# A hand-written order around the last attention tiles and the first expert blocks: two schedule strings rewritten

## The chip, the cores and the metric

The kernel runs on one core of one Trainium2 chip. The metric is the device time of one execution in microseconds; a kernel's time is the median of its runs.

## What is computed

The reference is one block of a Perceiver-like network in float32, on 64 sequences of 32 tokens of 256 features (2048 tokens), each sequence with its own context of 257 rows of 128 features. Cut to what matters:

```python
x = x + cross_attention(layernorm(x), ctx)       # 16 heads of 64; keys and values from ctx
x = x + self_attention(layernorm(x))             # 4 heads of 64, rotary angles, 32 tokens a sequence
x = x + experts(layernorm(x))                    # 8 experts, the best 2 of each token

# experts: scores = x @ Wr.T + br; top 2; their softmax weights, normalized to sum 1
# h = x @ Wl1[e]; y = (silu(h[:, :512]) * h[:, 512:]) @ Wl2[e]; out = weighted sum of the two y
```

## The kernel before

**Tiles.** The 2048 tokens are 16 tiles of 128 tokens, four sequences each. For every sequence, `cross_probs` computes scores, softmax and a transpose, in four steps (named `s` in the schedule). `cross_mix`, named `mix`, multiplies the probabilities of a pair of sequences with the context's values. The rest of a tile is a generator, `rest`: output of the cross attention, self-attention, routing. The generator yields at places where TensorE would have to wait for another engine, so that another piece of work can be put in between.

**The pipeline.** While tile t goes through scores and mixes, the `rest` of tile t-1 is called `near`, that of t-2 `far` and that of t-3 `late`. `ahead` computes the queries of tiles to come. A string for each sequence of a tile tells which generator makes its next step, word by word; `last_steps` holds the four strings of tile 15. After its last mix there is no tile left to compute scores for: `near` is then the rest of tile 15, `far` that of tile 14.

**Experts.** Each token goes to two of eight experts. `route` finds them and scatters the token's row into a DRAM tensor `routed` by indirect DMAs from GpSimd, two for a tile; the second waits for the first. Blocks of 128 rows of one expert are then gathered from `routed`. Six "early" blocks hold only rows that were routed by tile 12, so they can run while tiles 14 and 15 are still in their `rest`. `late_blocks` counts the rows of all tiles and lays out the late blocks (28 run for this input). A block has these units in the schedule:

- `x`, `prepared`: the gathered rows are transposed (by TensorE, L752, for early blocks and the first eight late ones), and VectorE forms gates and targets (L762 to L768).
- `a`, `first_half`: 8 matmul calls (L783), the halves that go through silu.
- `b`, `second_half`: 8 more; ScalarE's silu (L801), VectorE's product (L806).
- `c`, `combined`: 4 matmul calls (L818), bias and gate on VectorE (L823, L824), then an indirect DMA by GpSimd that adds the rows into `out` (L825).

The first layer's bias is read from the weights by L801 and L806, the second layer's by L823; weights stay in "lanes" of SBUF, two for early blocks (even blocks in lane 0, odd ones in lane 1) and three for late ones. After `c` of block b, SyncE issues the loads for block b + 2, under a condition that is true if the expert differs.

**What sets the order.** TensorE and SyncE (with its DMA queue) execute in the program's order, as the code writes it: `tc.manual_schedule(engines={SP, PE})`. VectorE, ScalarE and GpSimd execute in an order that a scheduler chooses when the program is built, and each of them in that order strictly. A reordering of the strings thus changes TensorE's order as written and the others' as the scheduler finds. PSUM has eight banks; `banks` gives out the one that was taken longest ago, and `a` holds its bank until `b`. The tiles `bxT` have two buffers, `y` four.

**Lines that come up.** L238 and L239: transposes on TensorE and their copies. L359, L363, L364, L371, L373: scores, maximum, exp, normalizing, transpose. L390 mix. L414, L428, L432, L438 output of the cross attention (L424 and L422 copy its middle). L221 to L231 layer norm, with a power on GpSimd (L228, `rstds` before self-attention, `rstdr` before routing). L448, L451 to L464 query, key and value and their rotation. L478, L485, L486, L494 to L503 scores and softmax of the self-attention, whose transposed probabilities are `diag`. L508, L516, L519, L522, L523 its output. L556 to L622 routing (`rex`, L587, is a power on GpSimd for the last two tiles, L619 their store to `out`). L647, L649 counts for the late blocks; `meta` (L908, L911, L918) tells SyncE which rows and weights to fetch.

Of the kernel before, what the change touches and what calls it, by code (L numbers as in the profile page):

```python
# [51 lines left out]
def block_kernel(  # L52
# [880 lines left out]
    def rotary_tables():  # L933
# [87 lines left out]
        "late ahead late s near s near s far s mix",  # L1021
    )
    last_steps = (
        "late far ahead s late far s s near s",
        "s near late far late s s s near ahead far mix ahead",
        "s s far s near s far",
        "s s near s near s mix far",
    )
    probs = {}
    seqs = [(t, b) for t in range(NT) for b in range(4)]  # L1030
# [19 lines left out]
    def iota(shape, pattern, base, by_partition, name):  # L1050
        it = const.tile([P] + shape, FP, name=name)
        nc.gpsimd.iota(
            it,
            pattern,
            base=base,
            channel_multiplier=by_partition,
            allow_small_or_imprecise_dtypes=True,
        )
        return it
# [21 lines left out]
    late = iota([LATE], [[1, LATE]], 0, 0, "late")  # L1081
# [38 lines left out]
    for n, (t, b) in enumerate(seqs):  # L1120
# [19 lines left out]
        if n + 1 < len(seqs):  # L1140
            t1, b1 = seqs[n + 1]
# [42 lines left out]
    def do(units):  # L1184
        for unit in units.split():
            if unit in work:
                next(work[unit], None)
            else:
                b = int(unit[1:])
                {  # L1190
                    "x": blocks.prepared,
                    "a": blocks.first_half,
                    "b": blocks.second_half,
                    "c": blocks.combined,
                }[unit[0]](b)
                if unit[0] == "c" and b + 2 < EARLY:
                    blocks.weights(b + 2, (0, 1))

    do("x0")
    blocks.gathered(EARLY - 1)  # L1200
    do("near far near far near a0 far x1 b0 near far near near x2 c0 near a1 near far b1 far")
    do("a2 near c1 far near x3 b2 a3 near c2 near x4 b3 near a4")
    late, total = late_blocks(done)
    do("c3")
    for b in range(3):
        late.gathered(b)
    do("b4 x5 a5 c4")
    late.weights(1, (0, 1))
    do("b5")
    late.prepared(0)  # L1210
    early_ones, blocks = blocks, late

# [107 lines left out]
```

## Time and profile before

| what | us |
|---|---|
| median of 3 runs (767.99 to 773.94) | 769.27 |
| the profiled execution, its own time | 770.71 |
| its span, first to last instruction | 768.9 |
| TensorE busy (8402 matmul instructions) | 726.0 |
| VectorE, ScalarE, GpSimd busy | 507.9, 394.0, 322.7 |

The profile is of one execution. Each call of a float32 matmul shows as two matmul records. In timeline rows the columns are start, duration, engine, line, operation, output and inputs, and in brackets the idle time before with what ended it. In rows of stretches the columns are the stretch, its length, the busy time (and instructions) of TensorE, its weight load, VectorE, ScalarE and GpSimd, the granted TensorE clock as a share of full speed, the DMA engines' busy share and GB/s. In the chain of work that ended last, each row is start, duration and what the end was waiting on at that time.

### The profile page before, as it was taken

Reading aid. Unit: us, or ns where it says so; the run is one execution under the profiler, and the core shown is the slowest. Engines: PE = TensorE matmul, PEld = TensorE weight load, DVE = VectorE, ACT = ScalarE, POOL = GpSimd, SP = SyncE. Lnnn points to the kernel's source line nnn. Section 1 sums busy time; section 2 is a strip of 40 time slices with the busy share of each in tenths; the row PEclk is TensorE's granted clock in tenths of the full one; section 3 lists DMA queues with packets and bytes.
Section 4 is the critical chain, followed back from the end, with each engine's and each line's share of the span. In section 5 each row is a group of like instructions: output and inputs, shape, how many; then the busy total and the mean of one; then the engine's idle time right before and its main releaser. Section 6 shows DMA issues by size and latency. Waiting matters only on the chain.

```text
span 768.9 us, 22412 instructions
## 1 busy us (share of the span) xinstructions
PE 726.0 (94%) x8402; PEld 616.3 (80%) x8402; DVE 507.9 (66%) x1968; ACT 394.0 (51%) x1168; POOL 322.7 (42%) x598
## 2 busy tenths in 40 slices
PE   8889999999999999999999999999698999999990
PEld 7668888787788878888787787887587999999990
DVE  4648777777886887787688777896267344454440
ACT  3756666666666676666666666764232222212210
POOL 2101072845648376474745738211135123322331
PEclk9999999999999999999999999999899999999996
DMA  8884323443333343233433334427212984485421
GB/s 247 229 213 106 90 78 88 122 113 93 92 87 112 88 134 100 77 94 98 120 107 86 91 88 115 124 84 259 105 11 60 329 300 56 51 251 114 57 36 22
DMA packets 62335, 90.85 MB, mean 118 GB/s; under 512 B 24144, under 2 KB 49104, under 8 KB 60688
## 3 DMA queue, kind: packets, MB, share of 16 engines
q1 hardware_dynamic: 55696, 80.32, 36.4%
q0 software_dynamic: 6528, 9.06, 6.6%
q8 instruction: 68, 1.11, 0.6%
q14 instruction: 43, 0.35, 0.2%
HBM read 113.76 MB, written 13.16 MB: 165 GB/s over the span
## 4 chain that ended last, share of the span: by engine, by line
PE 57%; POOL 13%; DVE 11%; DMA 9%; issue 5%; SPq 2%; ACT 1%; POOLq 0%; DVEq 0%
PE psum L783 13%; PE psum L359 9%; PE psum L390 8%; PE psum L818 6%; PE psum L432 5%; PE psum L334 5%; POOL rprod L544 4%; POOL rprod L539 4%; PE psum L448 3%; PE psum L313 3%; DMA out_x<-y_late,to_late 2%; SPq L101 2%; DVE prT L373 2%; DMA routed<-xr,rslots 2%; PE psum L414 1%
## 5 line engine op out<-in xcount | busy, mean ns | idle before, releaser
L364 ACT ACTIVATE pr<-psum,nmx 128x257 f32<-128x257 f32 x256 | 120.3, 474 | 90.2 <-DVE nmx L363 88.5
L359 PE MATMUL psum<-kvT,q 128*128 128x257 f32 x512 | 142.3, 399 | 3.4 <-DMA kvT<-in_ctx_t 2.3
L390 PEld LDWEIGHTS psum<-prT,kvA 32*128 32x128 f32 x4096 | 118.1, 187 | 11.2 <-issue 4.7
L390 PE MATMUL psum<-prT,kvA 32*128 32x128 f32 x4096 | 124.8, 274 | 0.5 <-ACT pr L364 0.4
L363 DVE TENSOR_REDUCE nmx<-psum 128x1 f32<-128x257 f32 x256 | 104.5, 414 | 30.3 <-PE psum L359 28.8
L371 ACT ACTIVATE pr<-pr,inv 128x256 f32<-128x256 f32 x256 | 114.7, 503 | 14.8 <-DVE inv L369 14.6
L359 PEld LDWEIGHTS psum<-kvT,q 128*128 128x128 f32 x512 | 89.6, 192 | 27.4 <-issue 7.9
L373 DVE STREAM_TRANSPOSE prT<-pr 128x512 f32<-128x512 f32 x128 | 89.9, 703 | 20.9 <-ACT pr L371 19.6
L825 POOL DMA_INDIRECT out_x<-y_late,to_late x28 | 43.6, 1558 | 109.3 <-DMA out_x<-y_late,to_late 43.0
L544 POOL TENSOR_TENSOR rprod<-rprod 128x128 f32<-128x128 f32 x192 | 75.3, 392 | 14.3
L539 POOL TENSOR_TENSOR rprod<-xr,wr_row 128x256 f32<-128x256 f32 x96 | 69.9, 728 | 7.5 <-DVE xr L231 0.8
L398 ACT COPY cT<-psum 128x512 f32<-128x512 f32 x64 | 34.2, 586 | 68.6 <-PE psum L390 68.6
L783 PE MATMUL psum<-bxT_late,lane 128*128 128x128 f32 x576 | 69.3, 275 | 0.0
L783 PEld LDWEIGHTS psum<-bxT_late,lane 128*128 128x128 f32 x576 | 68.2, 192 | 1.1 <-issue 0.2
L334 PE MATMUL psum<-xqT,xwq_sb 128*128 128x256 f32 x256 | 60.8, 381 | 0.5 <-ACT xqT L239 0.5
L432 PE MATMUL psum<-xwo_sb,ov 128*128 128x256 f32 x256 | 60.1, 382 | 0.5 <-DVE ov L424 0.2
L432 PEld LDWEIGHTS psum<-xwo_sb,ov 128*128 128x128 f32 x256 | 48.1, 190 | 9.1 <-DVE ov L424 2.9
L334 PEld LDWEIGHTS psum<-xqT,xwq_sb 128*128 128x128 f32 x256 | 48.6, 191 | 8.0 <-ACT xqT L239 0.7
L801 ACT ACTIVATE sag_late<-psum,lane 128x128 f32<-128x128 f32 x72 | 20.5, 368 | 63.9 <-PE psum L783 63.9
L364 ACT ACTIVATION_READ_ACCUMULATOR pr<-psum,nmx 128x1 f32 x256 | 50.9, 199 | 0.0
L611 POOL DMA_INDIRECT routed<-xr,rslots x32 | 33.0, 1032 | 41.0 <-DMA routed<-xr,rslots 23.7
L406 POOL TENSOR_TENSOR xb<-x,xbo_bc 128x256 f32<-128x256 f32 x16 | 11.6, 728 | 87.4 <-DVE x L438 62.6
(268 smaller groups left out, 1204.0 us busy)
## 6 DMA issues: line engine op xcount, KB each, us to landing
kvA<-in_ctx_a SPq DMA_DIRECT2D x256, 128.0 KB
lane<-in_wall SPq DMA_DIRECT2D x24, 1028.0 KB
lane<-in_wall SPq DMA_DIRECT2D x24, 640.0 KB
lane2a<-in_wall SPq DMA_DIRECT2D x10, 1028.0 KB
kvT<-in_ctx_t SPq DMA_DIRECT2D x64, 128.5 KB
lane2b<-in_wall SPq DMA_DIRECT2D x10, 640.0 KB
xg_late<-routed SPq DMA_DIRECT2D x80, 32.0 KB
x<-in_x SPq DMA_DIRECT2D x16, 128.0 KB
```

The source lines that it names most:

```text
L334: nc.tensor.matmul(pq[:, mm, :], xwq_sb[:, k, m * P : (m + 1) * P], xqT[:, k, :], start=(k == 0), stop=(k == 1),)
L359: nc.tensor.matmul(s, qb[:, g * P : (g + 1) * P], kvT, start=True, stop=True)
L363: nc.vector.tensor_reduce(nmx, s, AX.X, ALU.max, negate=True)
L364: nc.scalar.activation(pr[:, g, :], s, AF.Exp, bias=nmx, accum_out=sums[:, g : g + 1])
L371: nc.scalar.mul(pr[:, i, :ML], pr[:, i, :ML], inv[:, i : i + 1])
L373: nc.vector.transpose(prT[:, :, two, :], pr[:, two, :ML].rearrange("p g (c m) -> p c g m", c=MC))
L390: nc.tensor.matmul(psum[:, at + h, i * P : (i + 1) * P], values[n][r, c, :], prT[r, c, :, :].rearrange("p g n -> p (g n)"), start=(c == 0) ...
L432: nc.tensor.matmul(po, ov[:, m, :], xwo_sb[:, m, :], start=False, stop=(m == XH // 2 - 1))
L539: nc.gpsimd.tensor_tensor(prod, xr[:, 0:D], wr_rows[i], ALU.mult)
L544: nc.gpsimd.tensor_tensor(dst, prod[:, :n], prod[:, n : 2 * n], ALU.add)
L783: nc.tensor.matmul(self.ps[b][half][:, j, :].rearrange("p (c i) -> p c i", c=4), w[:, lo : lo + P], self.xTs[b][:, :, k, :], start=(k == 0 ...
L818: nc.tensor.matmul(py, g[:, j * P : (j + 1) * P], w[:, j * D : (j + 1) * D], start=(j == 0), stop=(j == 3),)
```

## The change

Two pieces of the hand-written order are rewritten: the strings of tile 15, and the sequence of chain steps and expert units after its last mix, up to the first late block. No operation is added or removed; nothing but the order differs.

```diff
     last_steps = (
-        "late far ahead s late far s s near s",
-        "s near late far late s s s near ahead far mix ahead",
-        "s s far s near s far",
-        "s s near s near s mix far",
+        "late late s ahead far s s far near s",
+        "near s late s late far near ahead far s mix ahead s",
+        "s far near s s far s",
+        "s near s s near s mix far",
     )
...
-    do("x0")
     blocks.gathered(EARLY - 1)
-    do("near far near far near a0 far x1 b0 near far near near x2 c0 near a1 near far b1 far")
-    do("a2 near c1 far near x3 b2 a3 near c2 near x4 b3 near a4")
+    do("far x0 near near near near far a0 far x2 x1 b0 near near near c0 near near near x3 far")
+    do("a1 a2 b1 far near c1 near b2 a3 near near b3 x4 near")
     late, total = late_blocks(done)
-    do("c3")
-    for b in range(3):
-        late.gathered(b)
-    do("b4 x5 a5 c4")
+    do("x5 c2 c3")
+    late.gathered(0)
+    do("a4")
+    late.gathered(1)
+    late.gathered(2)
+    do("b4 a5 b5 c4")
     late.weights(1, (0, 1))
-    do("b5")
     late.prepared(0)
     early_ones, blocks = blocks, late
```

Before, tile 14's self-attention and tile 15's alternate step by step, and the units a0 to b5 are spread between them; block 2's `c` comes before block 3's `b`. After, tile 15's steps are taken in runs of three or four, block 0's first half comes behind tile 14's L508, two blocks are transposed at once (x2 before x1), and the units c2 to b5 come in a row behind the counts for the late blocks.

More of the change, by code (lines that the diff above doesn't have):

```diff
@@ L1197, in do @@
                     blocks.weights(b + 2, (0, 1))
-    do("x0")
     blocks.gathered(EARLY - 1)
-    do("near far near far near a0 far x1 b0 near far near near x2 c0 near a1 near far b1 far")
-    do("a2 near c1 far near x3 b2 a3 near c2 near x4 b3 near a4")
+    do("far x0 near near far near far a0 far x2 x1 b0 near near near c0 near far near x3 far")
+    do("a1 a2 b1 far near c1 near b2 a3 near near b3 x4 near")
     late, total = late_blocks(done)
-    do("c3")
-    for b in range(3):
-        late.gathered(b)
-    do("b4 x5 a5 c4")
+    do("x5 c2 c3")
[4 more added lines that the diff above has]
+    do("b4 a5 b5 c4")
     late.weights(1, (0, 1))
-    do("b5")
     late.prepared(0)
```

## The prediction

> **What bounds the kernel now.** I read in this order: the page's slices, the chain that ended last, TensorE's (PE's) waits and timeline from 505 to 600 us, VectorE's (DVE's), and GpSimd's (POOL's) to the end.
>
> ```profile
> span 768.9 us, 22412 instructions
> ...
> PE   8889999999999999999999999999698999999990
> ...
> PE psum L508 <- DVE diag L503: 7.4, 1, 7.4
> ...
> 541.23 0.18 DVE L498 RECIPROCAL ainv<-asums 128x4 f32<-128x4 f32 x1
> ...
> 548.95 0.17 DVE L762 TENSOR_TENSOR gates_early<-xg_early,mine_early 128x8 f32<-128x8 f32 x1 [7.54 <-DMA xg_early<-routed]
> 549.03 0.28 DVE L499 TENSOR_TENSOR apr<-apr,ainv 128x128 f32<-128x128 f32 x1
> ...
> 550.87 1.12 PE L508 MATMUL psum<-diag,qkv 128*64 128x128 f32 x8 [7.42 <-DVE diag L503]
> ...
> 551.00:552.00 1.00, 1.00 (x9) 0.67 (x9) 0.64 (x5) 0.00 (x0) 0.24 (x1) 0.50 0.00 0
> 552.00:556.00 4.00, 4.00 (x21) 4.00 (x22) 0.56 (x2) 1.53 (x5) 0.32 (x1) 0.58 0.00 0
> ```
>
> PE is nearly full, with one hole: slice 29. PE waits 7.42 us for `diag`, the softmax of tile 14's self-attention. Its multiply (L499) was ready at 541.4, but DVE, in order, stood at the gates of early block 5, whose rows landed at 548.95. The last two lines (clock after the POOL column) show what follows: 1 us at 0.50 and 4 us at 0.58, so 0.50 + 1.68 = 2.2 us more. From 533.0 to 598.8, where the late blocks' matmuls start, the PE timeline's idle is 0.53 + 0.15 + 7.42 + 0.19 + 0.90 + 0.75 + 0.20 + 0.51 + 1.28 + 0.28 + 0.49 = 12.7 us. After 598.8 PE has no gap until the last block.
>
> ```profile
> 597.25 1.58 POOL L825 DMA_INDIRECT out_x<-y_early,to_early  x1 [2.96 <-DMA out_x<-y_early,to_early]
> 606.90 1.56 POOL L825 DMA_INDIRECT out_x<-y_early,to_early  x1 [8.07 <-DMA out_x<-y_early,to_early]
> 615.12 1.56 POOL L825 DMA_INDIRECT out_x<-y_late,to_late  x1 [6.66 <-DVE y_late L824]
> 623.92 1.56 POOL L825 DMA_INDIRECT out_x<-y_late,to_late  x1 [7.24 <-DMA out_x<-y_late,to_late]
> ...
> 608.51 0.35 DVE L824 TENSOR_SCALAR y_late<-y_late,gate_late 128x256 f32<-128x256 f32 x1
> ...
> 751.98 0.35 DVE L824 TENSOR_SCALAR y_late<-y_late,gate_late 128x256 f32<-128x256 f32 x1
> ...
> 748.80 5.71 DMA out_x<-y_late,to_late
> 754.55 0.71 issue
> 755.26 3.78 DMA out_x<-y_late,to_late
> ```
>
> PE does not end the kernel. Each scatter-add of an expert block into `out` waits for the one before to land. Late block 0's `y` is ready at 608.9 and its scatter starts at 615.12; block 27's at 752.3 and 759.79. Comparing all 28 pairs, none lags less than 6 us: from early block 4 (597.25) on, one unbroken chain sets the end. A step takes 4.55 us (744.21 to 748.80) when the queues are quiet and (623.92 - 606.90) / 2 = 8.5 us while expert weights stream, from about 598 to 631, and about 8 us for a step again near 683.
>
> **What the Trainium skill says.** "TensorE: Matmul & The Clock Gate", What's actually happening: the array falls to half clock after an idle window of about 3.4 us. The trace agrees: 0.50 after 7.42 us of idle. The holes I expect below are about 2 us, so I charge them no slow clock. "DMA: Bandwidth & Descriptors", Rules for kernel authors: an accumulating DMA must wait for an earlier one on the same bytes; that is the chain here, 4.55 us a step. Same page, Queues, rings and completion order: each DMA engine takes turns between queues by packets, so weights slow the scatters; 8.5 against 4.55 us agrees.
>
> **Part 1: tiles 14 and 15 (`last_steps`).** PE's work is the same; one score matmul pair of sequence 2 (L359, 0.45 us) goes behind the first mix of tile 15, and another ahead of tile 13's transposes, filling its 0.24 us gap. The mix (518.02) starts 0.7 us earlier. SP's last value loads wait for its first half ("SPq L101 <- PE psum L390", 9.7 us), and behind them stand a store, the `u` loads, lane 0's weights and the gathers of early blocks 0 to 4. The last of these that DVE waits for lands at 535.47, so this too moves by 0.7 us. Against it, ScalarE gets half of sequence 2's exp and normalizing (0.67 us and two of 0.46) after the mix. I estimate that the router's L556 then waits 1.2 us, but the second mix still starts earlier, since the old 0.91 us wait before L448 goes. Taken: 0.7 us gained; bounds -0.5 and 1.5.
>
> **Part 2: behind the last mix.** The order of the built program shows what the diff doesn't: on DVE the gates of block 5 now stand behind the four `diag` transposes and tile 15's L221. Times are those of before. Output projection ends 541.6; exp 540.9, sum, reciprocal, L499 to 541.7, L438 to 542.3, four L503 of 0.30 to 543.5. PE has a0 only behind L508: it waits 2.0 us. Then L508 (0.6), a0 (1.8), L522 (0.95), x2 and x1 (0.5), b0 (1.8) fill PE to 549.2. The gather still lands at 548.95, since its scatters, and SP's order, stand as before. Now tile 15's `xns` is behind it: 0.17 of gates, L224 and L226, POOL's power 0.57, L231 0.41: 550.8. PE waits 1.6 us. So 7.42 becomes 3.6.
>
> Next, each with rows of before:
> - xaT copy (0.37) before L448: 0.5 us;
> - c0 for L806: 0.25; the rotation of tile 15 (2.35 us on DVE, behind four L806): 0.6; qkT's copy (0.58) before L478: 0.5;
> - c1 for block 1's L806: 0.5. DVE has tile 14's routing ahead of it, with POOL's power (1.7 us) inside;
> - xrT's copy (ScalarE, 0.37) before L556: 0.7. `xr` of tile 15 itself comes sooner: before, its 2.66 us wait for POOL's rstdr;
> - c3 for block 3's L806: 0.7. That stands on DVE behind L588, which waits for POOL's rex15 (2.3 us), behind the store of tile 15, which waits for y1's scatter to land (5.1 us, the early median);
> - late block 0's gather: 1.8 us. From tile 15's rat to meta was 586.4 to 594.7, 8.3 us with y3 and four L806 inside; one more y costs 0.8, one L806 less saves 0.3. PE covers it with c3, a4, b4, a5, b5, c4 (10.6 us).
>
> Sum: 2.0 + 1.6 + 0.5 + 0.25 + 0.6 + 0.5 + 0.5 + 0.7 + 0.7 + 1.8 = 9.15 us of idle. The late blocks start 12.7 + 2.2 - 9.15 = 5.75 us earlier, 6.4 with part 1. ACT table loads stay three. SP's weights for block b + 2 still come after c of block b; c2 and c3 are later, and lane 1's load for block 5 stands behind y2, but the DMA share of before is low there, so I take the condition false and charge nothing; if it loads, a 1.67 MB fetch at 387 GB/s is 4.3 us.
>
> **Part 3: the scatters.** y4 is now behind three `gates_late` groups on DVE, the last waiting for late block 2's rows. Its scatter starts about 2.0 us after the late blocks' start; before, 1.55 ahead of it (597.25 against 598.8). The chain enters the weights' stream 3.5 us later. That loses 3.5 / 8.5 = 0.41 step, made up at 4.55 us: 1.9 us. Bounds: 0 (the step at 631.82 took 6.3 us, which leaves slack) and 3.5 (all of it). Net: 6.4 - 1.9 = 4.5 us.
>
> **Base.** The profiled execution took 770.71 us, 1.8 more than its span; the median shown is 769.27 (767.99 to 773.94). I take 4.5 from the median: 764.8.
>
> **Rivals.**
> A, more gain (0.22). Walking PE instruction by instruction puts late block 0 at 591.8, 7.0 before 598.8, against 5.75 by the sum; with 0.7 and the scatters' clash free: 7.7, so 761.6. For it: the slack at 631.82. Against: new orders rarely meet no new wait.
> B, the stall turned into others (0.20). POOL's y1 scatter (1.65) now stands ahead of rstdr15, and the wait for its landing ahead of rex15; at 8.9 instead of 5.1 us (the longest landing) 3.8 of the 6.4 go, leaving 2.6 - 1.9 = 0.7: 768.6.
> C, slower (0.13). The scatter chain loses not 0.41 but one whole contended step: 8.5 - 6.4 = 2.1 us lost, 771.4. It decides if one scatter fewer lands before the stream ends; from 6.4 us of loss on, the change is slower. For it: the end hangs on this chain alone, and c2 to c4 all move towards its start. Against: y5, at 4.4 us after the late start, keeps its place.
> That the change does not do what it says is out: DVE's order has moved.
>
> **Chances.** Forecast 0.45, A 0.22, B 0.20, C 0.13. The forecast's own range is 762 to 767; with part 1's bounds, A, B and C's body: 757 to 772. One per cent, 7.7 us, is about what a measurement here can tell: faster by more is half of A and the forecast's tail with a fully free clash, 0.27; slower needs C twice, 0.07; the rest, 0.66, is within.
>
> **What would show it.** Right: L508's wait falls to about 2 us, L238 of tile 15 waits 1 to 2, PE's clock stays near 1 there, the late blocks start near 592.4, block 4's scatter starts after them, and lags of the scatters rise. Wrong: a wait over 3 us anywhere from 533 to 592, block 3's L806 much later than 578, weights fetched for early blocks, or a scatter chain that is no longer unbroken.

## The result, and the profile after

| | median, us | runs from to | profiled execution: own time, span |
|---|---|---|---|
| before | 768.79 | 766.43 to 773.94 (10 runs) | 770.71, 768.9 |
| after | 761.09 | 754.51 to 765.17 (10 runs) | 760.11, 758.3 |

The ratio after to before is 0.9885, with an interval of 0.9855 to 0.9914: 1.15% faster (0.86 to 1.45%). This ratio is not the quotient of the two medians, which is 0.9900; the ratios below differ from theirs in the same way. The forecast was 764.8 with a range of 757 to 772; the gain of the medians is 7.7 us instead of 4.5, the size that rival A gave. Most of the chance (0.66) had been put within 1%; the measured gain lies just beyond it, with 1% inside its interval. One line of the diff shown earlier is miscopied: the added sequence reads `far x0 near near far near far a0 far x2 x1 b0 near near near c0 near far near x3 far`, so tile 14's steps stand between tile 15's in two more places, and tile 15's steps are taken there in runs of one to three, not of three or four.

The page of after: span, TensorE (PE) by slices, and the granted clock.

```profile
span 758.3 us, 22405 instructions
...
PE   8799999999999999999999999999799999999990
...
PEclk9999999999999999999999999999999999999996
```

Slice 29, a 6 before, is a 7 now, and the clock no longer dips there (before, its digit was an 8). Two stretches as single rows tell how much that is: from the counting matmul of tile 13's routing (L599), which stands right behind the last mix, to the first matmul of the late blocks (L783), first before, then after. Columns: stretch, length, busy time of PE, its weight load, VectorE (DVE), ScalarE, GpSimd (POOL), PE's clock, DMA share, GB/s.

```profile
533.06:598.80 65.74, 53.04 (x431) 46.61 (x431) 35.97 (x183) 18.62 (x46) 22.80 (x22) 0.95 0.30 91
```

```profile
530.78:588.59 57.81, 50.77 (x435) 44.42 (x432) 36.34 (x182) 18.43 (x46) 20.76 (x21) 1.00 0.35 106
```

The stretch is 7.93 us shorter. PE's idle went from 12.7 to 7.0 us, and the same matmuls take 50.8 instead of 53.0 us because the clock stays at 1.00. Next, VectorE's timeline and PE's, in time order, at the place of the old stall; in brackets the idle time before a row and what ended it.

```profile
539.58 0.29 DVE L499 TENSOR_TENSOR apr<-apr,ainv 128x128 f32<-128x128 f32 x1
...
547.26 0.17 DVE L762 TENSOR_TENSOR gates_early<-xg_early,mine_early 128x8 f32<-128x8 f32 x1 [5.38 <-DMA xg_early<-routed]
...
541.47 0.66 PE L508 MATMUL psum<-diag,qkv 128*64 128x128 f32 x8 [1.68 <-DVE diag L503]
548.92 0.44 PE L238 MATMUL psum<-ident,xns 128*128 128x128 f32 x2 [1.69 <-DVE xns L231]
```

VectorE still idles for block 5's rows (L762), now 5.4 us, but the softmax of tile 14 (L499) is done before it instead of behind it. So PE's wait at L508 is 1.68 instead of 7.42 us, and the eight matmul records take 0.66 instead of 1.12 us. The gates now hold back `xns` of tile 15, and PE waits 1.69 us there. All of PE's waits by source that the trace of after lists in the stretch:

```profile
PE psum L238 <- DVE xns L231: 1.7, 1, 1.7
PE psum L508 <- DVE diag L503: 1.7, 1, 1.7
PE psum L752 <- DMA xg_late<-routed: 1.1, 1, 1.1
PE psum L432 <- DVE ov L424: 0.9, 1, 0.9
PE psum L556 <- ACT xrT L239: 0.5, 1, 0.5
PE psum L448 <- ACT xaT L239: 0.5, 1, 0.5
PE psum L478 <- ACT qkT L239: 0.5, 1, 0.5
```

Behind the stretch these two traces hardly differ. With T for the start of the late blocks, T to the end of the span is 768.9 - 598.80 = 170.1 us before and 758.3 - 588.59 = 169.7 after. The scatters show why: GpSimd's timeline of after, at the start of the chain and at its end, with the last `y` of VectorE:

```profile
589.96 1.56 POOL L825 DMA_INDIRECT out_x<-y_early,to_early  x1 [5.24 <-DVE y_early L824]
598.77 1.55 POOL L825 DMA_INDIRECT out_x<-y_early,to_early  x1 [7.25 <-DVE y_late L824]
607.54 1.54 POOL L825 DMA_INDIRECT out_x<-y_late,to_late  x1 [7.22 <-DMA out_x<-y_early,to_early]
...
749.19 1.55 POOL L825 DMA_INDIRECT out_x<-y_late,to_late  x1 [3.03 <-DMA out_x<-y_late,to_late]
...
741.54 0.35 DVE L824 TENSOR_SCALAR y_late<-y_late,gate_late 128x256 f32<-128x256 f32 x1
```

Early block 4's scatter (589.96) starts 1.4 us after T; before it started 1.5 us ahead of T. Yet the last one starts 160.6 us after T, before 161.0. It stands 7.3 us behind the last `y` (before 7.5): the unbroken chain of scatters still sets the end, and in this pair of traces the later entry didn't lengthen it.

### The profile page after: what moved, and what is told of

Its sections match the earlier page's. It is cut to its first block, busy times and chain, and to the rows that moved or that the text cites. A ratio compares the mean times of both kernels' runs of the same rounds, so it can differ in the third digit from the quotient of the medians.

```text
span 758.3 us, 22405 instructions
## 1 busy us (share of the span) xinstructions
PE 723.4 (95%) x8402; PEld 613.9 (81%) x8402; DVE 508.3 (67%) x1968; ACT 393.6 (52%) x1168; POOL 322.4 (43%) x598
## 4 chain that ended last, share of the span: by engine, by line
PE 74%; DVE 9%; POOL 5%; ACT 4%; DMA 3%; issue 2%; SPq 0%; POOLq 0%; DVEq 0%
PE psum L783 14%; PE psum L390 12%; PE psum L359 12%; PE psum L334 7%; PE psum L432 7%; PE psum L818 6%; PE psum L313 3%; PE psum L414 3%; PE psum L448 3%; DMA out_x<-y_late,to_late 2%; POOL rprod L544 2%; PE psum L522 2%; POOL rprod L539 2%; PE psum L238 2%; ACT pr L371 2%
## 5 line engine op out<-in xcount | busy, mean ns | idle before, releaser
L390 PE MATMUL psum<-prT,kvA 32*128 32x128 f32 x4096 | 127.2, 274 | 0.8 <-ACT pr L364 0.4
L783 PE MATMUL psum<-bxT_late,lane 128*128 128x128 f32 x576 | 69.0, 275 | 0.0
L783 PEld LDWEIGHTS psum<-bxT_late,lane 128*128 128x128 f32 x576 | 68.1, 192 | 0.9
L432 PE MATMUL psum<-xwo_sb,ov 128*128 128x256 f32 x256 | 60.2, 382 | 1.2 <-DVE ov L424 0.9
L432 PEld LDWEIGHTS psum<-xwo_sb,ov 128*128 128x128 f32 x256 | 48.0, 190 | 10.0 <-DVE ov L424 3.6
L406 POOL TENSOR_TENSOR xb<-x,xbo_bc 128x256 f32<-128x256 f32 x16 | 11.6, 728 | 83.6 <-DVE x L438 62.2
```

The source lines that it names most:

```text
L390: nc.tensor.matmul(psum[:, at + h, i * P : (i + 1) * P], values[n][r, c, :], prT[r, c, :, :].rearrange("p g n -> p (g n)"), start=(c == 0) ...
L432: nc.tensor.matmul(po, ov[:, m, :], xwo_sb[:, m, :], start=False, stop=(m == XH // 2 - 1))
L783: nc.tensor.matmul(self.ps[b][half][:, j, :].rearrange("p (c i) -> p c i", c=4), w[:, lo : lo + P], self.xTs[b][:, :, k, :], start=(k == 0 ...
```

## The experiments

Theories: **S**, the gain is the one VectorE order at block 5's gates; **O**, it is the sum of the new sequence's orders; **E**, the chain of scatters sets the end and so decides how much of an earlier T reaches it. Each group of runs shared one chip and the kernel before on it (763.45 us for the first four, 765.97 for the last four), so medians are compared within a group.

**Part 1 alone**: before, with the four strings of the change's `last_steps`.

```diff
-        "late far ahead s late far s s near s",
+        "late late s ahead far s s far near s",
 ...
```

> Only the strings of tile 15 (part 1); the steps behind the last mix stay as before. Main theory (most of the gain comes from L508 no longer standing behind the gather of block 5 on VectorE): the gathers land about 0.7 to 1 us earlier, the wait of L508 stays near 7.4 us, total gain 0.5 to 1.5 us, not to be told from before. Rival (tile 15's order carries the gain): 5 us or more faster, and the wait of L508 falls.

Measured: 763.73 us, ratio 0.9988 (0.9963 to 1.0013): no difference that can be told, and so none of the 5 us of the rival. PE's timeline shows the old stall in place, with its slow clock:

```profile
545.94 1.12 PE L508 MATMUL psum<-diag,qkv 128*64 128x128 f32 x8 [6.66 <-DVE diag L503]
```

In the profile the last mix does come sooner: from the count for the early blocks (L647, "the early count") to L599 it is 26.52 us, before 28.07, after 26.70. From L599 to T it is 65.52 against 65.74. A gain of 1.5 us, 0.2%, lies inside the interval of the ratio, so its worth at the end stays undecided.

**Part 2 alone**: after, with the old `last_steps` (the diff above in reverse).

> Only the steps behind the last mix (part 2); the strings of tile 15 stay as before. Main theory: 6 to 9 us faster than before, L508 waits 1.5 to 2.5 us instead of 7.4, late blocks start 7 to 9 us earlier. Rival (tile 15's order carries the gain): under 3 us faster. Rival (the two parts need each other): both parts alone well under half.

Measured: 756.82 us, ratio 0.9902 (0.9867 to 0.9937), 6.6 us faster: nearly the whole effect, and not to be told from all of it. L599 to T is 55.25 us, 2.6 us less than in after. PE's waits at `xns` (0.2 instead of 1.7 us) and at L432 (none instead of 0.9) make most of the difference:

```profile
PE psum L508 <- DVE diag L503: 1.7, 1, 1.7
PE psum L752 <- DMA xg_late<-routed: 1.3, 1, 1.3
...
PE psum L238 <- DVE xns L231: 0.2, 1, 0.2
```

The rows of block 5 reach VectorE 13.8 us after L599 here and 16.5 us after it in after. So in this pair of traces what part 1 wins up to the mix is lost again behind it. One half has a pattern: L432 waits 0.5 to 1.5 us in every run with part 1's strings, and 0.2 us or not at all in every run without them. Why the gather stands further behind L599 in after is open: part 1 alone does not do it (15.6 us, before 15.9), and with the order of after and one scatter left out it is 15.7. The wait at `xns` was 1.3 us in the repeat of after below.

**One VectorE order alone**: before, with all of TensorE's and SyncE's order as it was. Only block 5's gates and targets are pinned to their place in the program, so that the scheduler puts them behind the late blocks' plan (`meta`, L908) instead of ahead of L499.

```diff
-            nc.vector.tensor_tensor(gates, xw[:, :NE], self.mine[:, b, :], ALU.mult)
+            (tc.keep_in_program_order if self.name == "early" and b == EARLY - 1 else id)(
+                nc.vector.tensor_tensor(gates, xw[:, :NE], self.mine[:, b, :], ALU.mult))
 ... (the copy of the targets, L766, in the same way)
```

> The kernel before, with one thing changed: the three VectorE instructions that form block 5's gates and targets are kept in program order, so they stand behind the late blocks' plan instead of ahead of L499. TensorE's, ScalarE's, GpSimd's and SyncE's orders are the same as before. Main theory (the wait of L508 behind the gather, 7.4 us and 2.2 us of slow clock after it, is the loss): L508 waits under 2 us, late blocks start 6 to 9 us earlier, 5 to 8 us faster. Rival (the new order of the expert units behind the counts brings the gain): TensorE meets the same total of waits a little later, under 3 us faster.

Measured: 757.03 us, ratio 0.9916 (0.9878 to 0.9953), 6.4 us faster, as good as part 2. In the traces TensorE, ScalarE and GpSimd execute the same instructions in the same order as before, and VectorE's order differs by these three alone. The timeline of VectorE, of PE, and the whole stretch as one row:

```profile
541.04 0.29 DVE L499 TENSOR_TENSOR apr<-apr,ainv 128x128 f32<-128x128 f32 x1
...
585.18 0.16 DVE L762 TENSOR_TENSOR gates_early<-xg_early,mine_early 128x8 f32<-128x8 f32 x1
...
542.98 0.66 PE L508 MATMUL psum<-diag,qkv 128*64 128x128 f32 x8
...
532.80:589.20 56.40, 51.17 (x431) 44.76 (x431) 36.02 (x182) 18.62 (x46) 22.69 (x22) 1.00 0.34 104
```

L508 of tile 14 doesn't wait at all, since the old order has block 0's first half (`a0`) ahead of it. The stretch is 9.3 us shorter than before with none of the change's words. So the one VectorE order is enough for the effect, as S has it; beyond it the rest of part 2's reordering shows 1.15 us in the profiles (56.40 against 55.25) and nothing in the medians. The reverse, the new orders with the gates still ahead of L499, was not run, so that nothing else could have filled the hole is not shown.

**The same pin in the changed kernel.**

> The changed kernel with block 5's gates kept in program order. Main theory: tile 15's layer norm no longer waits for the gather, the 1.7 us wait of its transposes goes, the rest stays: 1 to 2 us faster than the changed kernel, 8 to 10 faster than before. Rival (that wait is cover for the next, such as xaT's copy, the gates' plan or the late gather): no difference from the changed kernel.

The edit is that of the pin, made in after. Measured: 755.10 us, ratio 0.9882 (0.9844 to 0.9919), 8.4 us faster than before. The ratio of after is 0.9885, so the 1 to 2 us over the changed kernel are not shown in the time. In the trace `xns` no longer waits for the gather:

```profile
537.55 0.66 PE L508 MATMUL psum<-diag,qkv 128*64 128x128 f32 x8 [1.68 <-DVE diag L503]
543.15 0.38 PE L238 MATMUL psum<-ident,xns 128*128 128x128 f32 x2
```

L599 to T is 55.61 us, 2.2 less than in after, and L647 to L599 keeps part 1's 26.38. What stays at L508 is the price of the new sequence, which has `a0` behind L508 and not ahead of it, where it had covered L503.

**After on the second chip**, unchanged, as the yardstick for the group.

> The changed kernel once more, beside the other kernels of this call on one chip. If part 1 brings nothing to the whole (its 1.4 us before the mix are spent in a longer wait for block 5's gather), it stands to before as part 2 alone did: ratio 0.990, 7 to 8 us. If part 1 adds its 1.4 us in full: 0.988.

Measured: 758.07 us, ratio 0.9884 (0.9839 to 0.9930), span 756.0 us. The ratio of the result repeats. Its interval holds both forecasts, 0.990 and 0.988, so this does not decide what part 1 adds. T is at 588.68, and GpSimd's last scatter is here:

```profile
746.96 1.55 POOL L825 DMA_INDIRECT out_x<-y_late,to_late  x1 [3.04 <-DMA out_x<-y_late,to_late]
```

That is 158.3 us after T and 4.1 us behind the last `y`; T to the end is 167.3 us. In the first trace of the same kernel these were 160.6, 7.3 and 169.7. Two executions of one kernel, on two chips, thus differ by 2.4 us behind T, in the chain.

**The pin, and a0 ahead of L508.**

```diff
-    do("far x0 near near far near far a0 far x2 x1 b0 near near near c0 near far near x3 far")
+    do("far x0 near near far near a0 far far x2 x1 b0 near near near c0 near far near x3 far")
```

> The changed kernel with block 5's gates in program order and block 0's first half (a0) ahead of tile 14's L508. Main theory: the 1.7 us wait of L508 is filled by a0 and tile 15's transposes no longer wait for the gather: 2 to 4 us faster than the changed kernel, late blocks 3 us earlier. Rival (L522 then waits for oT's copy, which moves behind a table load of 1.28 us and a silu on ScalarE): 0 to 2 us.

Measured: 756.89 us, ratio 0.987 (0.9823 to 0.9918), the lowest ratio of the versions that do the whole computation. PE's waits in it:

```profile
PE psum L752 <- DMA xg_late<-routed: 1.1, 1, 1.1
PE psum L432 <- DVE ov L424: 1.0, 1, 1.0
...
PE psum L508 <- DVE diag L503: 0.3, 1, 0.3
```

L508's wait goes from 1.7 to 0.3 us and L599 to T is 586.25 - 531.17 = 55.1 us, 3.1 less than in after on this chip (58.1). The rival's wait, L522 for oT's copy, came as well and is 0.5 us. The medians differ by 1.2 us only, and the two intervals overlap nearly whole: better in the profile, not shown in the time.

**One scatter fewer**, for the chain.

```diff
-            nc.gpsimd.indirect_dma_start(
+            (self.name, b) != ("early", 5) and nc.gpsimd.indirect_dma_start(
```

> The changed kernel without the scatter-add of early block 5 into the output; its matmuls and its y are still computed. Theory that the chain of scatter-adds sets the end: every later scatter starts one step earlier in the weights' stream, the end comes about 4.5 us (one quiet step) earlier, 3 to 6. Rival (TensorE, or the last blocks' y, sets the end): under 1 us.

Measured: 755.17 us, ratio 0.9852 (0.9809 to 0.9895), 2.9 us below after on the same chip. GpSimd's last scatter, and VectorE's last `y`:

```profile
744.22 1.55 POOL L825 DMA_INDIRECT out_x<-y_late,to_late  x1 [2.93 <-DVE y_late L824]
...
743.39 0.35 DVE L824 TENSOR_SCALAR y_late<-y_late,gate_late 128x256 f32<-128x256 f32 x1
```

The last scatter now waits for its `y`, 0.5 us behind it, not for its predecessor. T to the end is 752.9 - 588.31 = 164.6 us, 2.7 less than in after on this chip. Once the chain is a step shorter, the last `y` sets the end, so less than a step comes through. This fits E (3 to 6 us foreseen) better than the rival (under 1 us); but the intervals of the two ratios overlap, and 2.7 us is hardly more than what two executions of after differ by.

**Two chains**: the odd late blocks add into a second tensor, so each chain has half of the late steps.

```diff
-                out=out[:, :],
+                out=(side if self.name == 'late' and b % 2 else out)[:, :],
 ...
+    [load(side[i * P : (i + 1) * P, :], none[:, :D]) for i in range(NT + 1)]
```

> The changed kernel with the scatter-adds of the odd late blocks going to a second tensor that is not added to the output, so two chains of scatters run side by side; 17 zero stores of 128 KB for it are added at the start. Theory that the chain sets the end: the scatters no longer lag by 6 us or more, the last one starts about 1 to 2 us after its y, and the stretch from the late blocks' first matmul to the end of the span falls from 169.7 us by 4 to 7. Rival (TensorE sets the end): that stretch stays within 1 us.

Measured: 769.84 us, ratio 1.0037 (1.0019 to 1.0056): slower. PE's waits in the first 80 us name a reason, and the last scatter shows the other half:

```profile
PE psum L359 <- DMA kvT<-in_ctx_t: 7.9, 1, 7.9
PE psum L390 <- DVE x L438: 3.7, 1, 3.7
...
760.88 1.55 POOL L825 DMA_INDIRECT side<-y_late,to_late  x1 [2.73 <-DVE y_late L824]
```

The 17 stores that clear the second tensor stand ahead of the context loads on SyncE's queue. The early count comes at 520.88 instead of 503.93 us, 17 us late, which the run's total shows. VectorE's order near 60 us also differs from that of after, so the stores need not be all of it. From T on, it is 769.9 - 606.38 = 163.5 us, against 167.3 in after on this chip and 169.7 on the other, and the last scatter lags its `y` by 0.3 us (a fall of 4 to 7 us was foreseen). So the serial chain costs about 4 to 6 us at the end in these executions of after. A form of this without the stores at the start wasn't tried.

## Why the prediction was right, and where it was off

**The bound and the stall: right.** The hole of 7.42 us was block 5's gates ahead of L499 on VectorE, and the slow clock came with it. After shows 1.68 us at L508 (2.0 foreseen), 1.69 at `xns` (1.6), and a clock of 1.00. The pin alone shows that moving the gates is enough to close the hole. The other signs came too: block 4's scatter starts behind T, and the first late block's scatter lags its `y` by 8.9 instead of 6.3 us. T itself is at 588.6, sooner than the 592.4 foreseen. That holes of about 2 us carry no slow clock was in part luck: it held in this stretch of after and of all other runs without the old stall but one: with two chains the wait at `xns` was followed by 3 us at half clock (last section).

**The sum of new waits: too large.** Foreseen 9.15 us, measured 6.8 in the waits of this table.

| wait | foreseen | measured |
|---|---|---|
| L508, xns | 2.0, 1.6 | 1.7, 1.7 |
| L448, L478, L556 | 0.5, 0.5, 0.7 | 0.5, 0.5, 0.5 |
| c0, rotation, c1, c3 | 0.25, 0.6, 0.5, 0.7 | none, 0.1, none, none |
| late block 0's rows | 1.8 | 1.1 |
| L432 | not in the sum | 0.9 |

The four waits for VectorE behind a queue of other work (2.05 us together) all but vanish in the trace of after, and against them L432's, which comes with part 1, had been put at nothing. With all of PE's idle, 7.0 us, in place of 9.15 the prediction's own sum gives 12.7 + 2.2 - 7.0 = 7.9 us for part 2, and the stretch is 7.93 us shorter.

**Part 1: right in the profile, its worth at the end open.** 0.7 us foreseen, 1.4 seen up to the last mix, with L556's wait at 0.9 us (1.2 foreseen) and the old one before L448 gone, as foreseen. Behind the mix the traces of after and of part 2 alone differ by more than that the other way (waits at `xns` and L432); with the pin in, the trace keeps part 1's gain. The medians leave it undecided.

**The scatters: no loss in the traces, open in the runs.** Foreseen were a chain that enters 3.5 us later and loses 1.9 us; in the traces it enters 2.9 us later and loses nothing. (The quiet step's own times give 4.59 us instead of the 4.55 stated; the 1.9 stays.) The start of the scatters after T (e for early blocks, l for late ones), and the last:

| us after T | e4 | e5 | l0 | l1 | l2 | l3 | l27 |
|---|---|---|---|---|---|---|---|
| before | -1.5 | 8.1 | 16.3 | 25.1 | 33.0 | 39.3 | 161.0 |
| after | 1.4 | 10.2 | 18.9 | 26.8 | 33.7 | 38.5 | 160.6 |

The stream of expert weights ends at the same distance from T in both. The DMA share, the last column but one, falls at T + 30; two rows each for the 3 us before T + 30 and the 3 us after it, before and then after.

```profile
625.80:628.80 3.00, 3.00 (x27) 2.95 (x26) 1.40 (x7) 0.71 (x3) 0.00 (x0) 1.00 1.02 355
628.80:631.80 3.00, 3.00 (x24) 2.85 (x23) 0.78 (x2) 0.80 (x4) 0.00 (x0) 1.00 0.58 123
```

```profile
615.59:618.59 3.00, 3.00 (x27) 2.95 (x26) 1.40 (x7) 0.72 (x3) 1.36 (x1) 1.00 0.98 362
618.59:621.59 3.00, 3.00 (x24) 2.85 (x23) 0.78 (x2) 0.79 (x4) 0.00 (x0) 1.00 0.61 131
```

A chain that enters later has less of the stream before it, and the steps l1 to l3 come out shorter (11.7 us against 14.2). The prediction counted this as a fraction of a step, which would give back 1.35 of 2.9 us; these two traces give all of it. That this is the rule is not shown: single steps under the stream vary between about 7 and 10 us, and the pinned kernels, with entries of -1.5 and 1.4 us, reach l3 at 37.8 and 39.7.

The times of the runs also leave room for a loss. From the early count to T the traces get shorter by 9.3 us in after, 10.6 with part 2 alone and 9.4 with the pin in before; the medians gain 7.7, 6.6 and 6.4. Part of this may be chance, since the intervals of the ratios are 4.5 to 6 us wide, but a loss behind T like the 1.9 us foreseen fits the runs as well as none does. The runs without a trace are not split at T.

**Rivals.** A was right in size and nearly in its reasons: the clash was free, and the walk along TensorE's order (7.0 us for part 2) came closer than the sum. B is out: no wait of PE in the stretch of after names GpSimd as what ended it, and none reaches 2 us. C's mechanism, a whole step of the chain, may exist: with the pin in before, T to the end is 164.8 us, and there one more scatter is done ahead of the second stream of weights (late block 12's starts 79.8 us after T, before 84.2). But the later entry didn't set it off: T to the end was 169.4 to 170.1 us in the traces of before, part 1 alone, part 2 alone and after, and 167.3 in the repeat of after.

**Profile and median.** The profiled executions differ by 10.6 us, the medians by 7.7. Of the 10.6, 0.9 us was there at the early count (504.99 against 504.08), ahead of anything that differs, 1.4 lies before L599, 7.9 behind it, 0.4 in the tail. Single executions spread at both ends: the early count, with the same order ahead of it, lies between 500.7 and 505.0 us in all runs but the one with two chains, and T to the end differs by 2.4 us between two executions of after. A difference between two profiles ahead of the early count or behind T is thus no evidence here.

## What to carry to other kernels

An instruction that waits for a DMA on an engine that executes in order holds everything queued behind it; look for what was ready behind it before rewriting another engine's order, since here one pinned instruction group gave a ratio of 0.9916 where the two rewritten schedules gave 0.9885, with overlapping intervals. When stages are brought forward, look at what they wait for next: part 1's 1.4 us met new waits at L432 and at the gather. Where a serial chain of DMAs sets the end, don't read what an earlier stage is worth from one pair of traces: the same kernel's tail took 169.7 and 167.3 us here.

## What the runs showed of the hardware

- TensorE's clock fell with a hole of 7.4 us (0.50 for 1 us behind it, then 0.58 for 4 us) and likewise in part 1 alone with one of 6.66 us (0.50, then 0.53). Holes of 1.7 us left it at 1.00 in after, but that is no rule: with two chains, in the same order of TensorE, a wait of 1.27 us at `xns`, and one of 0.46 us behind it, were followed by 3 us at 0.50 (the clock is the third column from the right):

```profile
565.40 0.44 PE L238 MATMUL psum<-ident,xns 128*128 128x128 f32 x2 [1.27 <-DVE xns L231]
...
567.50:570.50 3.00, 3.00 (x6) 1.69 (x5) 2.14 (x7) 0.00 (x0) 0.00 (x0) 0.50 0.00 0
```

  Near 27 us a hole of 1.5 us did the same in the pinned kernel after (0.50 from 27.8 to 31.2 us), and one of 1.8 us in after did not. The prediction took an idle window of about 3.4 us from the Trainium skill's "TensorE: Matmul & The Clock Gate", What's actually happening. The long holes agree with it; the short ones show that a hole under 2 us can be enough in one execution and not in another. What decides it is open.
- A scatter-add chain's step under full DMA load is about 8.5 us and its quiet step about 4.6. With two chains on two tensors the next scatter of the other chain started 1.84 us after the first (626.24 and 628.08), while expert weights streamed, and the first chain's own next one at 634.68: the waiting is between scatters of one tensor, not in the issue.
- With seventeen stores of 128 KB ahead of the context loads on a queue the early count came 17 us later. TensorE shows 11.6 us of that as its two longest waits; from 40 to 60 us its clock was 0.83, in after on the same chip 1.00.
